# A decoder's start: the first batch of a group handled alone, the rest behind it, in one fixed order

## The chip, the cores and the metric

The kernel runs on one core of a Trainium2 chip. The metric is the device time of one execution in microseconds, as the median of several runs. Five engines work beside each other: TensorE (PE; its weight loads are PEld), VectorE (DVE), ScalarE (ACT), GpSimd (POOL) and SyncE (SP), which here only issues transfers.

## The reference

One decoder layer over 16 batches of 128 tokens with 256 features, all in float32. Each of its three parts is added to its own input:

```
x = x + attn(layernorm(x))          # differential attention, 16 heads
x = x + xattn(layernorm(x), ctx)    # cross attention to ctx, gelu behind it
x = x + ffn(layernorm(x))           # one shared expert, 16 routed ones, best 2 of 16

def attn(x):
    q, k, v = split(x @ W_qkv)      # q, k as 2 * 16 heads of 8; v as 16 heads of 16
    a1 = softmax(q1 @ k1.T * 8**-0.5) @ v
    a2 = softmax(q2 @ k2.T * 8**-0.5) @ v
    o = a1 - lam * a2               # lam from four small vectors
    o = o * rsqrt(mean(o * o) + eps) * subln_w * (1 - lambda_init)
    return o @ W_proj + b_proj
```

The layer norm has no weights: a token's features less their mean, over the root of their variance.

## The kernel before

The 16 batches are 4 groups of 4. A tile has 128 partitions; for a token tile these are the 128 tokens of a batch. `xs[g]` holds group g of x, with one tile in it for each batch.

The start handles group 0 as a whole. `wqkv` is loaded from ScalarE's queue, the four batches of `xs[0]` and then `xs[1]` from SP's. `layernorm` makes each batch's mean and variance on VectorE (`bn_stats`, `bn_aggr`, L124 and L125), adds epsilon (L127), raises the four variances to the power -1/2 on GpSimd (L128), and normalizes batch by batch with a `tensor_scalar` on VectorE (L134) into `xn`. `turns` transposes `xn` on TensorE (L152) and copies it to `xnT`, features by tokens: one half with ScalarE (L155), the other with VectorE (L157). `project` multiplies with the weights `wqk`, whose columns ScalarE has put into another order before (L220). It makes the keys kT (n = 1, copied out by VectorE, L253) and the queries qT (n = 0, scaled and copied out by ScalarE, L255), for each half e of the features. Keys then go by transfers into `kb`, where each head has its own columns between zeros (L260), and into `k3` (L269). Queries go into `qb` (L264), for group 0 from ScalarE's queue. `values` makes `v` (L276, L283). `kb`, `qb`, `v` and `k3` exist twice, for even and odd groups; each is filled with zeros or ones first: `kb0` by VectorE (L206), `kb1` by ScalarE out of the tile `zeros` (L455), the others by GpSimd's `memset` (L207, L210 to L212, L427, L453, L459).

Behind the start runs the loop over steps k. Step k computes for batch k the row maxima of the scores: TensorE's `pq` (L294) and a `tensor_reduce` of VectorE for each (L299), eight of them to a batch. Step k + 1 turns the maxima to a row (`pn`, L307; `nr`, L309) and loads it into `qb` (L311). Step k + 2 makes the probabilities (`pk`, L325, and the exponential, L331), and later steps weigh the values, subtract, normalize and project back. The next group's layer norm, transposes and projections are spread over the four steps of the group before it. Behind the loop come the cross attention, which partly overlaps it, and the two kinds of experts.

Two things set the order on an engine. From `begin = traced()`, just ahead of the loop (L746), `in_order` (called at L1164) ties each instruction on TensorE, VectorE, ScalarE and GpSimd to the one before it in the text. Ahead of `begin` a scheduler picks the order; there `pin` (`keep_in_program_order`) holds some instructions in place, and one fill has a dependency of its own:

```
        filled = pin(nc.gpsimd.memset(ones, 1.0))
        tc.add_manual_dep(
            filled.ins, last_ln.ins.name,
            mybir.DependencyInfo(mybir.DependencyClass.Sync, mybir.DependencyReason.DATA),
            reason="long fills stay behind the first group's normalization",
        )
```

Of the kernel before, what the change touches and what calls it, by code (L numbers as in the profile page):

```python
# [9 lines left out]
F32 = mybir.dt.float32  # L10
# [33 lines left out]
def tile_decoder(  # L44
# [53 lines left out]
    def cons(shape, name, pool=const):  # L98
        return pool.tile(shape, F32, tag=name, name=name)
# [2 lines left out]
        return ap[g * GB : (g + 1) * GB].rearrange("b p d -> p b d")  # L102


    wqkv = cons([P, NC_, 3 * D], "wqkv", aconst)
    nc.scalar.dma_start(out=wqkv, in_=w_qkv.rearrange("(c p) e -> p c e", p=P))
    xs = []
# [7 lines left out]
    make_identity(nc, ident)  # L115
    mhalf = cons([P, 1], "mhalf")
    nc.gpsimd.memset(mhalf, -0.5)
    def statistics(pool, xg, parts=1):

        mv = pool.tile([P, GB, 2], F32, tag="ln_mv", name="ln_mv")  # L120
        rs = pool.tile([P, GB], F32, tag="ln_rs", name="ln_rs")
        for b in range(GB):
            st = pool.tile([P, 6], F32, tag="ln_st", name="ln_st")
            nc.vector.bn_stats(st, xg[:, b, :])  # L124
            nc.vector.bn_aggr(mv[:, b, :], st)  # L125
            if b == GB - 1:
                nc.vector.tensor_scalar(rs, mv[:, :, 1], EPS, None, ALU.add)  # L127
                nc.gpsimd.tensor_tensor(rs, rs, mhalf.to_broadcast([P, GB]), ALU.pow)  # L128
            if (b + 1) % (GB // parts) == 0:
                yield mv, rs  # L130
# [9 lines left out]
    def layernorm(pool, xg, xn):  # L140

        return normalize(xg, xn, *next(statistics(pool, xg)))

    def bank(shape, name):
        return ps.tile(shape, F32, tag="ps", name=name)
# [27 lines left out]
    def traced():  # L173
        return len(nc.cur_bb.bb.instructions)
# [25 lines left out]
    with actx:  # L200
# [3 lines left out]

        zeros = cons([P, 4 * D], "zeros", aconst)
        nc.vector.memset(kbs[0], 0.0)  # L206
        pin(nc.gpsimd.memset(qbs[0], 0.0))  # L207

        def blank_values(n):
            pin(nc.gpsimd.memset(vs[n], 0.0))  # L210
            nc.gpsimd.memset(vs[n][:, :, :, VD : VD + 1], 1.0)
            pin(nc.gpsimd.memset(k3s[n], 1.0))  # L212

        blank_values(0)


        wqk = aconst.tile([P, NC_, 2, D], F32, tag="wqk", name="wqk")
        for n in range(2):
            for c in range(NC_):
                nc.scalar.copy(  # L220
                    wqk[:, c, n, :].rearrange("p (t d j) -> p t d j", d=HD, j=4),
                    wqkv[:, c, n * D : (n + 1) * D].rearrange(
                        "p (t j d) -> p t d j", d=HD, j=4
                    ),
                )

        def normed_tile():
            return share.tile([P, GB, D], F32, tag="xn", name="xn", bufs=1)

        def biased(g):  # L230

            pin(nc.gpsimd.tensor_tensor(
                xs[g], xs[g], bproj_r.unsqueeze(1).to_broadcast([P, GB, D]), ALU.add
            ))

        def turns(g, xn):
            xnT = share.tile([P, NC_, GT], F32, tag="xnT", name="xnT", bufs=1)
            transposed(xn, xnT)
            qT = share.tile([P, NC_, GT], F32, tag="qT", name="qT")
            kT = share.tile([P, NC_, GT], F32, tag="kT", name="kT")  # L240
            return xnT, (qT, kT)

        def project(g, xnT, qk, n, e):

            pp = bank([P, GT], "pp")
            for c in range(NC_):
                nc.tensor.matmul(  # L247
                    pp, lhsT=wqk[:, c, n, e * P : (e + 1) * P], rhs=xnT[:, c, :],
                    start=(c == 0), stop=(c == NC_ - 1),
                )  # L250
            dst = qk[n]
            if n:
                nc.vector.tensor_copy(dst[:, e, :], pp)  # L253
            else:
                nc.scalar.activation(dst[:, e, :], pp, AF.Copy, scale=HD**-0.5)  # L255
            queue = nc.scalar if g == 0 and n == 0 else nc.sync
            kb, qb = kbs[g % 2], qbs[g % 2]
            if n:
                for j in range(4):
                    queue.dma_start(out=kb[j::4, e, j, :], in_=dst[j::4, e, :])  # L260
            else:
                for j in range(4):
                    m = 4 * e + j
                    queue.dma_start(out=qb[m % 3 + 1 :: 4, m, :], in_=dst[j::4, e, :])  # L264
# [6 lines left out]
        def values(g, xnT, b2):  # L271
            pv = bank([P, 2, D], "pv")
            for i in range(2):
                b = 2 * b2 + i
                for c in range(NC_):
                    nc.tensor.matmul(  # L276
                        pv[:, i, :],
                        lhsT=xnT[:, c, b * P : (b + 1) * P],
                        rhs=wqkv[:, c, 2 * D : 3 * D],
                        start=(c == 0),  # L280
                        stop=(c == NC_ - 1),
                    )
            nc.scalar.copy(  # L283
                vs[g % 2][:, 2 * b2 : 2 * b2 + 2, :, 0:VD],
                pv.rearrange("p i (h d) -> p i h d", h=H),
            )

        def maxima(b, c, qT, nm):

            g, i = divmod(b, GB)  # L290
            for t in range(4):
                rows = slice(32 * t, 32 * t + 32)
                pq = bank([P, 4, P], "pq")
                nc.tensor.matmul(  # L294
                    pq, lhsT=qT[rows, c, i * P : (i + 1) * P],
                    rhs=kbs[g % 2][rows, c, :, i * P : (i + 1) * P],
                    start=True, stop=True,
                )
                nc.vector.tensor_reduce(  # L299
                    nm[:, NM * t + 4 * c : NM * t + 4 * c + 4], pq, AX.X, ALU.max, negate=True  # L300
                )
# [98 lines left out]
        def output(b, oT):  # L400
# [6 lines left out]
                )  # L407
            nc.vector.tensor_tensor(xs[g][:, i, :], py, xs[g][:, i, :], ALU.add)

        xn_next = normed_tile()  # L410
        last_ln = layernorm(share, xs[0], xn_next)
        xnT, first = turns(0, xn_next)
        for e in range(NC_):
            for n in (1, 0):
                project(0, xnT, first, n, e)
        for e in range(NC_):
            keys_by_key(0, first[1], e)
        for b2 in range(GB // 2):
            values(0, xnT, b2)


        bproj_r = row(b_proj, D, "bproj_r", aconst)
# [1 line left out]
        wproj = cons([P, NC_, D], "wproj", aconst)  # L424
        wcol = cons([P, 1], "wcol")
        ones = cons([P, P], "ones")
        filled = pin(nc.gpsimd.memset(ones, 1.0))  # L427
        tc.add_manual_dep(
            filled.ins, last_ln.ins.name,
            mybir.DependencyInfo(mybir.DependencyClass.Sync, mybir.DependencyReason.DATA),  # L430
            reason="long fills stay behind the first group's normalization",
        )

        lprod = cons([P, 2, HD], "lprod")
        lsum = cons([P, 2], "lsum")
# [11 lines left out]
        def projection():  # L447

            pin(nc.vector.tensor_scalar(wcol, wcol, 1.0 - LAMBDA_INIT, None, ALU.mult))
            nc.vector.tensor_scalar(wproj, wproj, wcol, None, ALU.mult)  # L450


        pin(nc.gpsimd.memset(zeros, 0.0))  # L453
        for c in range(NC_):
            pin(nc.scalar.copy(  # L455
                kbs[1][:, c].rearrange("p j n -> p (j n)"), zeros[:, 0:1].to_broadcast([P, 4 * GT])
            ))
        blank_values(1)
        pin(nc.gpsimd.memset(qbs[1], 0.0))  # L459
        biased(0)  # L460


        lower = cons([P, P], "lower")
        pin(nc.gpsimd.memset(lower, 1.0))
        nc.gpsimd.affine_select(
            out=lower, in_=lower, pattern=[[1, P]], compare_op=ALU.is_gt, fill=0.0,
            base=0, channel_multiplier=-1,
        )
        eidx = cons([P, NE], "eidx")
        pin(nc.gpsimd.iota(  # L470
            eidx, pattern=[[1, NE]], base=-NE, channel_multiplier=0,
            allow_small_or_imprecise_dtypes=True,
        ))
        carry = cons([P, NE, B], "carry")
        pin(nc.gpsimd.memset(carry, 1.0))
        nc.gpsimd.memset(carry[:, :, 0:1], 0.0)
        tstart = cons([P, NTILE], "tstart")
        pin(nc.gpsimd.iota(
            tstart, pattern=[[P, NTILE]], base=0, channel_multiplier=0,
            allow_small_or_imprecise_dtypes=True,  # L480
        ))

        ebias_r = cons([P, NE], "ebias_r")
        rw = cons([P, NC_, NE], "rw")
# [258 lines left out]

        begin = traced()  # L746
        qk = {0: first}
        nms, probs, ots, as_, diffs, os_ = {}, {}, {}, {}, {}, {}
        for k in range(B + 5):
            g, i = divmod(k, GB)  # L750
            more = k < B and g + 1 < NG
            if k < B:
                nms[k] = work.tile([P, 4 * NM], F32, tag="nm", name="nm")
                maxima(k, 0, qk[g][0], nms[k])
            if k - 1 in nms:
                maxima_rows(k - 1, nms.pop(k - 1))
                for to, of in later.pop(k, ()):
                    load(out=to, in_=of)
# [24 lines left out]
                biased(g + 1)  # L783
            if k < B:
                maxima(k, 1, qk[g][0], nms[k])
            planned(k, 1)
            if k - 3 in ots:
                averaged(ots.pop(k - 3), as_[k - 3][:, 1])
# [457 lines left out]
```

## Time and profile before

| | |
|---|---|
| median of 11 runs | 613.0 us (611.55 to 615.17) |
| the profiled execution | 614.19 us |
| its span, first to last instruction | 612.5 us |
| mean granted TensorE clock | 0.976 |
| PE, PEld | 575.6 us (94%), 386.5 us (63%) |
| DVE, ACT, POOL busy | 304.8 us (50%), 205.9 us (34%), 176.0 us (29%) |

The times of the steps are those of the profiled execution, counted from its first instruction. A line of the timeline gives the start, the duration of a merged run of like instructions, the engine, the line of the kernel, the operation, the tile written and the tiles read, the shapes, the number of instructions (x), and in brackets how long the engine was idle before it and what ended that. A duration starts when the instruction's waits are over. A record of a transfer on a queue (SPq, ACTq) is its issue and not its flow. A float32 matmul of the program shows as two records.

### The profile page before, as it was taken

Reading aid. Unit: us, or ns where it says so; the run is one execution under the profiler, and the core shown is the slowest. Engines: PE = TensorE matmul, PEld = TensorE weight load, DVE = VectorE, ACT = ScalarE, POOL = GpSimd, SP = SyncE. Lnnn points to the kernel's source line nnn. Section 1 sums busy time; section 2 is a strip of 40 time slices with the busy share of each in tenths; the row PEclk is TensorE's granted clock in tenths of the full one; section 3 lists DMA queues with packets and bytes.
Section 4 is the critical chain, followed back from the end, with each engine's and each line's share of the span. In section 5 each row is a group of like instructions: output and inputs, shape, how many; then the busy total and the mean of one; then the engine's idle time right before and its main releaser. Section 6 shows DMA issues by size and latency. Waiting matters only on the chain. (4 is left out here: it accounts for less than half of the span.)

```text
span 612.5 us, 10607 instructions
## 1 busy us (share of the span) xinstructions
PE 575.6 (94%) x3820; PEld 386.5 (63%) x3820; DVE 304.8 (50%) x714; ACT 205.9 (34%) x468; POOL 176.0 (29%) x142
## 2 busy tenths in 40 slices
PE   3989989998999999979799999999899999999996
PEld 1435655654565556666475667465399999988455
DVE  5386866677768773724654543611232232221553
ACT  2325535564454555442425421101122222220110
POOL 8240242244223442541302000676000000004571
PEclk9969989999999999979799999999999999999999
DMA  3311343421104020003300440222499889812352
GB/s 120 111 54 63 101 190 152 154 97 36 54 21 141 3 80 1 2 1 102 105 0 1 118 158 0 77 105 95 130 324 279 280 275 271 252 44 78 102 152 90
DMA packets 58872, 67.65 MB, mean 110 GB/s; under 512 B 8512, under 2 KB 51520, under 8 KB 58816
## 3 DMA queue, kind: packets, MB, share of 16 engines
q1 hardware_dynamic: 55088, 57.21, 28.8%
q0 software_dynamic: 3072, 8.39, 4.3%
q10 hardware_dynamic: 656, 1.31, 0.6%
q8 instruction: 33, 0.54, 0.4%
q14 instruction: 23, 0.19, 0.1%
HBM read 41.73 MB, written 18.61 MB: 99 GB/s over the span
## 5 line engine op out<-in xcount | busy, mean ns | idle before, releaser
L299 DVE TENSOR_REDUCE nm<-pq 128x4 f32<-128x512 f32 x128 | 79.4, 681 | 26.2 <-PE pq L294 26.2
L331 ACT ACTIVATE pr<-pk 128x384 f32<-128x384 f32 (+1 forms) x192 | 70.5, 475 | 19.3 <-PE pk L325 18.8
L1128 POOL DMA_INDIRECT yg<-yd,si x32 | 31.1, 973 | 143.6 <-DMA yd<-yr 128.6
L1101 PE MATMUL pu<-xrT,w 128*128 128x128 f32 x576 | 70.2, 275 | 0.0
L1101 PEld LDWEIGHTS pu<-xrT,w 128*128 128x128 f32 x576 | 67.3, 192 | 0.1
L379 POOL TENSOR_TENSOR rms<-rms,mhalf 128x16 f32<-128x16 f32 x16 | 46.6, 2910 | 71.5 <-DVE rms L378 71.5
L879 PE MATMUL pa<-xT,w 128*128 128x512 f32 x128 | 60.4, 594 | 0.0
L879 PE MATMUL pb<-xT,w 128*128 128x512 f32 x128 | 60.1, 592 | 0.0
L893 PE MATMUL py<-w,h 128*128 128x256 f32 x256 | 55.9, 379 | 0.0
L884 ACT ACTIVATE act<-pa 128x512 f32<-128x512 f32 x32 | 19.1, 597 | 105.2 <-PE pa L879 100.7
L885 DVE TENSOR_TENSOR h<-act,pb 128x512 f32<-128x512 f32 x32 | 21.9, 687 | 63.7 <-PE pb L879 52.7
L893 PEld LDWEIGHTS py<-w,h 128*128 128x128 f32 x256 | 48.6, 190 | 7.9 <-issue 1.4
L325 PE MATMUL pk<-qb,k 32*128 32x384 f32 (+1 forms) x384 | 48.9, 497 | 0.4 <-DVE a L360 0.4
L294 PE MATMUL pq<-kb,qT 32*128 32x512 f32 x256 | 48.6, 640 | 0.6 <-DVE a L360 0.4
L1108 DVE TENSOR_TENSOR hT<-ract,pu 128x256 f32<-128x256 f32 x36 | 15.1, 420 | 63.8 <-ACT ract L1106 63.8
L1063 POOL DMA_INDIRECT xd<-xn,si x32 | 31.1, 972 | 44.3 <-DVE si L1036 34.9
L879 PEld LDWEIGHTS pb<-xT,w 128*128 128x128 f32 x128 | 24.3, 190 | 30.6 <-issue 30.1
L879 PEld LDWEIGHTS pa<-xT,w 128*128 128x128 f32 x128 | 23.7, 190 | 24.6 <-issue 23.9
L247 PE MATMUL pp<-xnT,wqk 128*128 128x512 f32 x64 | 34.9, 682 | 4.0 <-DVE xnT L157 3.5
L1114 PE MATMUL pyr<-w,hT 128*128 x144 | 37.0, 380 | 0.0
L325 PEld LDWEIGHTS pk<-qb,k 32*128 32x128 f32 x384 | 23.3, 185 | 19.7 <-issue 7.1
L349 ACT COPY ot<-po 128x512 f32<-128x512 f32 x32 | 18.8, 586 | 50.1 <-PE po L342 50.1
(157 smaller groups left out, 793.8 us busy)
## 6 DMA issues: line engine op xcount, KB each, us to landing
w<-in_L_ffn_routed_w_dram SPq DMA_DIRECT2D x88, 256.0 KB
xd<-zeros SPq DMA_DIRECT2D x11, 512.0 KB
xr<-xd SPq DMA_DIRECT2D x36, 128.0 KB
yd<-yr SPq DMA_DIRECT2D x36, 128.0 KB
w<-in_L_ffn_shared_w_dram SPq DMA_DIRECT2D x12, 256.0 KB
kb<-kT SPq DMA_DIRECT2D x32, 64.0 KB
k<-kT SPq DMA_DIRECT2D x32, 64.0 KB
ctx<-in_ctx_dram SPq DMA_DIRECT2D x4, 512.0 KB
```

The lines of the kernel that those rows point to most:

```text
L247: nc.tensor.matmul(pp, lhsT=wqk[:, c, n, e * P : (e + 1) * P], rhs=xnT[:, c, :], start=(c == 0), stop=(c == NC_ - 1),)
L294: nc.tensor.matmul(pq, lhsT=qT[rows, c, i * P : (i + 1) * P], rhs=kbs[g % 2][rows, c, :, i * P : (i + 1) * P], start=True, stop=True,)
L299: nc.vector.tensor_reduce(nm[:, NM * t + 4 * c : NM * t + 4 * c + 4], pq, AX.X, ALU.max, negate=True)
L325: nc.tensor.matmul(pk, lhsT=k3s[g % 2][rows, k, i * P : (i + 1) * P], rhs=qbs[g % 2][rows, heads, i * P : (i + 1) * P], start=True, stop=True,
L331: nc.scalar.activation(pr[:, 0:n, :], pk, AF.Exp)
L379: nc.gpsimd.tensor_tensor(rms, rms, mhalf.to_broadcast([P, H]), ALU.pow)
L879: nc.tensor.matmul(pp, lhsT=w[:, c, fs], rhs=xT[g][:, c, :], start=(c == 0), stop=(c == NC_ - 1),)
L893: nc.tensor.matmul(py[:, i, :], lhsT=hs[u][:, f, b * P : (b + 1) * P], rhs=units[u][2][:, f, :], start=(u == 0 and f == 0), stop=(u == NS ...
L1063: i = nc.gpsimd.indirect_dma_start(out=xd[:, :], out_offset=bass.IndirectOffsetOnAxis(ap=slots[n][:, t : t + 1], axis=0), in_=xns[t // GB] ...
L1101: nc.tensor.matmul(pu[:, n, f, :], lhsT=w12[:, c, n, f * P : (f + 1) * P], rhs=xrT[:, c, :], start=(c == 0), stop=(c == NC_ - 1),)
L1114: nc.tensor.matmul(py, lhsT=hT[:, f, :], rhs=w3[:, bass.ds(e * NC_ + f, 1), :], start=(f == 0), stop=(f == NC_ - 1),)
L1128: nc.gpsimd.indirect_dma_start(out=yg, out_offset=None, in_=yd[:, :], in_offset=bass.IndirectOffsetOnAxis(ap=slots[n][:, t : t + 1], axis=0),)
```

## The change

`begin` moves to the first load, so that all instructions on the four engines, those of the start too, stand in the order of the text. The start is written anew in that order. `first_normed([0])` normalizes batch 0 with a power of its own; it is transposed, and eight 128 wide matmuls make its keys and queries in one bank `pp`; its keys are loaded into `kb` by four transfers that hold both halves. `first_normed([1, 2, 3])` follows, and then the transposes and the keys of the three batches, 384 tokens wide. Their queries (`project(0, xnT, first, 0, e, P)`) and the values of the group come inside step 0 of the loop, behind the score matmuls of batch 0. Of the fills, that of `v0` stands behind the power of batch 0, and those of `k30`, `qb0`, `ones` and `zeros` behind the power of the other three; those of the odd tiles (`other_half`) are issued in step 0, the bias of group 0 is added in step 2, and the routing's constants are made in step 4. The dependency of `ones` on the last normalization is gone.

```diff
+    begin = len(nc.cur_bb.bb.instructions)
     wqkv = cons([P, NC_, 3 * D], "wqkv", aconst)
...
-        pin(nc.gpsimd.memset(qbs[0], 0.0))
...
-        def project(g, xnT, qk, n, e):
+        def project(g, xnT, qk, n, e, at=0):
...
         xn_next = normed_tile()
-        last_ln = layernorm(share, xs[0], xn_next)
-        xnT, first = turns(0, xn_next)
+        xnT = share.tile([P, NC_, GT], F32, tag="xnT", name="xnT", bufs=1)
+        first = tuple(
+            share.tile([P, NC_, GT], F32, tag=name, name=name) for name in ("qT", "kT")
+        )
+
+        def first_normed(bs):
+            mv = share.tile([P, GB, 2], F32, tag="ln_mv", name="ln_mv")
+            rs = share.tile([P, GB], F32, tag="ln_rs", name="ln_rs")
+            for b in bs:
+                st = share.tile([P, 6], F32, tag="ln_st", name="ln_st", bufs=2)
+                nc.vector.bn_stats(st, xs[0][:, b, :])
+                nc.vector.bn_aggr(mv[:, b, :], st)
+            part = slice(bs[0], bs[-1] + 1)
+            nc.vector.tensor_scalar(rs[:, part], mv[:, part, 1], EPS, None, ALU.add)
+            nc.gpsimd.tensor_tensor(
+                rs[:, part], rs[:, part], mhalf.to_broadcast([P, len(bs)]), ALU.pow
+            )
+            for b in bs:
+                nc.vector.tensor_scalar(
+                    xn_next[:, b, :], xs[0][:, b, :], mv[:, b, 0:1], rs[:, b : b + 1],
+                    ALU.subtract, ALU.mult,
+                )
+
+        first_normed([0])
+        weights_ordered(1)
+        pt = bank([P, NC_, P], "pt")
+        for c in range(NC_):
+            nc.tensor.transpose(pt[:, c, :], xn_next[:, 0, c * P : (c + 1) * P], ident)
+        nc.scalar.copy(xnT[:, :, 0:P], pt)
+        weights_ordered(0)
+        blank_values(0)
+        first_normed([1, 2, 3])
+        pp = bank([P, 2, NC_, P], "pp")
+        for n in (1, 0):
+            for e in range(NC_):
+                for c in range(NC_):
+                    nc.tensor.matmul(
+                        pp[:, n, e, :], lhsT=wqk[:, c, n, e * P : (e + 1) * P],
+                        rhs=xnT[:, c, 0:P], start=(c == 0), stop=(c == NC_ - 1),
+                    )
+        nc.vector.tensor_copy(first[1][:, :, 0:P], pp[:, 1])
+        for j in range(4):
+            load(out=kbs[0][j::4, :, j, 0:P], in_=first[1][j::4, :, 0:P])
+        nc.scalar.activation(first[0][:, :, 0:P], pp[:, 0], AF.Copy, scale=HD**-0.5)
+        for c in range(NC_):
+            pt = bank([P, GB - 1, P], "pt")
+            for b in range(1, GB):
+                nc.tensor.transpose(
+                    pt[:, b - 1, :], xn_next[:, b, c * P : (c + 1) * P], ident
+                )
+            copies = nc.vector.tensor_copy if c else nc.scalar.copy
+            copies(xnT[:, c, P:].rearrange("p (b t) -> p b t", b=GB - 1), pt)
         for e in range(NC_):
-            for n in (1, 0):
-                project(0, xnT, first, n, e)
+            project(0, xnT, first, 1, e, P)
+        nc.gpsimd.memset(k3s[0], 1.0)
+        nc.gpsimd.memset(qbs[0], 0.0)
         for e in range(NC_):
             keys_by_key(0, first[1], e)
-        for b2 in range(GB // 2):
-            values(0, xnT, b2)
...
-        filled = pin(nc.gpsimd.memset(ones, 1.0))
-        tc.add_manual_dep(
-            filled.ins, last_ln.ins.name,
-            mybir.DependencyInfo(mybir.DependencyClass.Sync, mybir.DependencyReason.DATA),
-            reason="long fills stay behind the first group's normalization",
-        )
+        nc.gpsimd.memset(ones, 1.0)
+        nc.gpsimd.memset(zeros, 0.0)
...
+        def other_half():
+
+            nc.gpsimd.memset(k3s[1], 1.0)
+            for c in range(NC_):
+                nc.scalar.copy(
+                    kbs[1][:, c].rearrange("p j n -> p (j n)"),
+                    zeros[:, 0:1].to_broadcast([P, 4 * GT]),
+                )
+            nc.gpsimd.memset(qbs[1], 0.0)
+            blank_values(1)
...
-        begin = traced()
         qk = {0: first}
...
                 maxima(k, 0, qk[g][0], nms[k])
+            if k == 0:
+                project(0, xnT, first, 0, 0, P)
...
                 maxima(k, 1, qk[g][0], nms[k])
+            if k == 0:
+                project(0, xnT, first, 0, 1, P)
+                values(0, xnT, 0)
+                values(0, xnT, 1)
+                other_half()
+            elif k == 2:
+                biased(0)
+            elif k == 4:
+                routing_constants()
```

More of the change, by code (lines that the diff above doesn't have):

```diff
@@ L206, in tile_decoder, with weights_ordered @@
         nc.vector.memset(kbs[0], 0.0)
-        pin(nc.gpsimd.memset(qbs[0], 0.0))
         def blank_values(n):
-            pin(nc.gpsimd.memset(vs[n], 0.0))
+            nc.gpsimd.memset(vs[n], 0.0)
             nc.gpsimd.memset(vs[n][:, :, :, VD : VD + 1], 1.0)
-            pin(nc.gpsimd.memset(k3s[n], 1.0))
-        blank_values(0)
         wqk = aconst.tile([P, NC_, 2, D], F32, tag="wqk", name="wqk")
-        for n in range(2):
+        def weights_ordered(n):
             for c in range(NC_):
@@ L241, in turns @@
             return xnT, (qT, kT)
-        def project(g, xnT, qk, n, e):
-            pp = bank([P, GT], "pp")
+        def project(g, xnT, qk, n, e, at=0):
+            pp = bank([P, GT - at], "pp")
             for c in range(NC_):
                 nc.tensor.matmul(
-                    pp, lhsT=wqk[:, c, n, e * P : (e + 1) * P], rhs=xnT[:, c, :],
+                    pp, lhsT=wqk[:, c, n, e * P : (e + 1) * P], rhs=xnT[:, c, at:],
                     start=(c == 0), stop=(c == NC_ - 1),
@@ L252, in project @@
             if n:
-                nc.vector.tensor_copy(dst[:, e, :], pp)
+                nc.vector.tensor_copy(dst[:, e, at:], pp)
             else:
-                nc.scalar.activation(dst[:, e, :], pp, AF.Copy, scale=HD**-0.5)
+                nc.scalar.activation(dst[:, e, at:], pp, AF.Copy, scale=HD**-0.5)
             queue = nc.scalar if g == 0 and n == 0 else nc.sync
@@ L259, in project @@
                 for j in range(4):
-                    queue.dma_start(out=kb[j::4, e, j, :], in_=dst[j::4, e, :])
+                    queue.dma_start(out=kb[j::4, e, j, at:], in_=dst[j::4, e, at:])
             else:
@@ L450, in projection, with routing_constants @@
             nc.vector.tensor_scalar(wproj, wproj, wcol, None, ALU.mult)
[L453 to L460, printed above, removed]
-        lower = cons([P, P], "lower")
[L464 to L468, printed above, removed]
+        def other_half():
[7 more added lines that the diff above has]
+            blank_values(1)
+        lower = cons([P, P], "lower")
         eidx = cons([P, NE], "eidx")
[L470 to L473, printed above, removed]
         carry = cons([P, NE, B], "carry")
-        pin(nc.gpsimd.memset(carry, 1.0))
-        nc.gpsimd.memset(carry[:, :, 0:1], 0.0)
         tstart = cons([P, NTILE], "tstart")
[L478 to L481, printed above, removed]
+        def routing_constants():
+            nc.gpsimd.memset(lower, 1.0)
+            nc.gpsimd.affine_select(
+                out=lower, in_=lower, pattern=[[1, P]], compare_op=ALU.is_gt, fill=0.0,
+                base=0, channel_multiplier=-1,
+            )
+            nc.gpsimd.iota(
+                eidx, pattern=[[1, NE]], base=-NE, channel_multiplier=0,
+                allow_small_or_imprecise_dtypes=True,
+            )
+            nc.gpsimd.memset(carry, 1.0)
+            nc.gpsimd.memset(carry[:, :, 0:1], 0.0)
+            nc.gpsimd.iota(
+                tstart, pattern=[[P, NTILE]], base=0, channel_multiplier=0,
+                allow_small_or_imprecise_dtypes=True,
+            )
         ebias_r = cons([P, NE], "ebias_r")
```

## The prediction

> **What bounds the kernel now.** I read the page first: the chain that ended last and the slices.
>
> ```profile
> PE pu L1101 11%; PE pyr L1114 5%; PE py L893 5%; PE pb L879 3%; PE pa L879 3%; PE pxt L1090 1%; DMA xr<-xd 0%; DVE x L1134 0%; DVE x L899 0%; SPq L1080 0%
> ...
> PE   3989989998999999979799999999899999999996
> DVE  5386866677768773724654543611232232221553
> ```
>
> The chain is TensorE work back to 436 us and is lost there, so it doesn't reach the stage that is edited. From the second slice on TensorE is nearly always busy, and its instructions stand in one fixed order. What starts late at the beginning therefore ends late, and the question is only how many microseconds the first 43 us gain or lose. So next came the timeline of that stage, engine by engine.
>
> ```profile
> 8.76 2.52 DVE L134 TENSOR_SCALAR xn<-x,ln_mv,ln_rs 128x256 f32<-128x256 f32 x4 [1.24 <-POOL ln_rs L128]
> ...
> 25.18 4.82 PE L294 MATMUL pq<-kb,qT 32*128 32x512 f32 x24
> ...
> 26.34 2.48 DVE L299 TENSOR_REDUCE nm<-pq 128x4 f32<-128x512 f32 x4 [5.53 <-PE pq L294]
> ```
>
> The first group is normalized by 11.28, TensorE works without a gap from 10.4 to 25.2 (transposes, 16 projection matmuls of 0.85, later 0.43 us, 3.62 us of values), and only then comes the first score matmul, `pq`, at T = 25.18. From the first `tensor_reduce` at 26.34 to 40.2 VectorE never waits: it is the bound there. So the whole kernel moves with T, unless something new ends later behind it.
>
> **What the change could give.** Of the TensorE work ahead of T it moves 3.62 us of values and three quarters of the query projections (8 records at 0.43, so 2.6 of 3.4 us) behind the first reduces, where VectorE is the bound and TensorE has room. It also lets the first batch's keys load alone. T would come earlier if the normalization were done as early as now. I don't think it is, because of the next rows.
>
> ```profile
> 8.70 0.19 POOL L211 MEMSET v<- 128x64 f32 x1
> 8.78 1.39 POOL L212 MEMSET k<- 128x1536 f32 x1
> 11.34 0.20 POOL L427 MEMSET ones<- 128x128 f32 x1 [1.17 <-DVE xn L134]
> ```
>
> A normalizing `tensor_scalar` takes 0.40 us, four in a row 1.37. The first one of the kernel took 1.56: it began at 8.76 and ended at 10.32, 0.15 after GpSimd's fill ended (8.78 + 1.39 = 10.17). The same once more, without a fill:
>
> ```profile
> 299.07 2.41 DVE L134 TENSOR_SCALAR xn<-x,ln_mv,ln_rs 128x256 f32<-128x256 f32 x4
> ...
> 298.02 2.34 POOL L612 TENSOR_TENSOR x<-x,ctx 128x1024 f32<-128x1024 f32 x1
> ```
>
> Four took 2.41 instead of 1.37; GpSimd ended at 300.36, and 300.36 + 0.15 + 3 x 0.32 = 301.47 is their end. So these instructions stand still while GpSimd works. What if GpSimd's next instruction waits for nothing?
>
> ```profile
> 33.38 0.27 DVE L127 TENSOR_SCALAR ln_rs<-ln_mv 128x4 f32<-128x4 f32 x1
> ...
> 31.14 2.34 POOL L232 TENSOR_TENSOR x<-x,bproj_r 128x1024 f32<-128x1024 f32 x1 [11.96 <-DMA bproj_r<-in_L_attn_b_proj_dram]
> 33.42 0.20 POOL L464 MEMSET lower<- 128x128 f32 x1
> ```
>
> GpSimd's add ended at 33.48 and its next fill had begun at 33.42, 0.06 before. VectorE's small instruction (0.17 elsewhere) ended at 33.65, 0.03 after the fill; where one such was held by a single add (295.87 to 296.82) it ended 0.03 after that. So it came in behind both. At 8.76, too, the fill at 8.70 handed over to the one at 8.78. Two hand-overs in two went to GpSimd, though both lay within 0.1 us of VectorE's start.
>
> **The change part by part**, in the times of the profiled execution.
>
> *Batch 0 alone.* Its statistics start at 5.11 as now (its load and the `kb` fill end there). Aggregate, add and hand-over as in the rows of now (0.45, 0.22, 0.32) put the power on GpSimd at 6.10. The power took 1.05 for 4 columns and 2.91 for 16, so 0.155 a column: 0.58 for one, to 6.68. Behind it GpSimd has the fill of `v0` (1.80), begun 0.06 early, so the normalization of batch 0 ends at 6.62 + 1.80 + 0.15 = 8.57. Nothing waits for it yet.
>
> *Batches 1 to 3.* Statistics at a pitch of 0.53 (28.74, 29.29): the third aggregate at 8.5 + 1.06 + 0.45 = 10.0, the add at 10.2, the power at 10.55 for 0.89, to 11.45. GpSimd's next instructions in the new order are `k30`, `qb0`, `ones`, `zeros`, `k31`, `qb1`, `v1`, and none of them waits for anything: the wait of `ones` for the last normalization, which shows above as 1.17 us, is what the diff takes out, and the fills of `k31`, `qb1`, `v1` stand in one row with it. From start to start they take, by the rows of now, 1.34 + 3.45 + 0.15 + 0.89 + 1.34 + 3.45, and `v1` 1.80 to its end: 12.42. Only then does GpSimd wait for itself. If the hand-overs go as the two above, the three normalizations stand from 11.5 to 11.4 + 12.4 = 23.8 and end at 24.0, 24.3 and 24.6, against 11.28 now.
>
> *What hangs on that.* VectorE's order puts the copy of batch 0's keys (done by TensorE since about 10) behind these three, so batch 0 isn't alone at all: copy 24.6 to 25.0 (0.42, the row of L1092). Four loads of `kb` on SP's queue: 2.46 as at 17.13, to 27.45. Landing: at least 0.8 (the traffic of the load issued at 17.13 is over at 18.5), at most 1.95 (`xr<-xd` in the chain); I take the middle, 28.9. Beside it six transposes, two copies and four 384 wide projections at 0.64 a record, cold, end at 28.2, hidden under the landing by 0.7. T = 28.9, which is 3.7 later than now.
>
> *Behind T.* ScalarE now has everything there: queries of e = 0 from T + 2.6 (scores 1.2, projection 1.3 before it), four DMA issues (2.7, as at 19.09), queries and issues of e = 1 to T + 8.9, two value copies (1.1), the two `kb1` fills (3.7): the maxima row `nr` goes out at T + 13.7 instead of T + 7.6. Its four loads issue to T + 16.9 and land at about T + 18.4, while the first `pk` stood at T + 17.6: 0.8 lost. The other edits cost nothing: SP has 4 issues more (2.5 us) but is through with `k3` and `bproj_r` by about T + 10, before `nr`; the adds of the bias and the routing constants move to steps 2 and 4, where GpSimd waited 22.7 us for `o` (L371), and the first user of that `x` comes at step 5. If that cover were gone it would be the 2.3 and 1.2 us that they take.
>
> Sum: 3.7 + 0.8 = 4.5 later. The profiled execution took 614.19 for a span of 612.5; it becomes 618.7. The median of the runs is 613.0, 1.2 below it, so 617.5. The landing (0.6 either way), `nr` (0 to 2) and the clock further down (its half rate stretches at 88, 269 and 300 us can shift, about 1) make 615 to 620.
>
> The Trainium skill, SBUF — State Buffer, section "Who interferes with whom", says that of a VectorE instruction in a two port mode and a GpSimd instruction the first to issue has the shared pair for its whole instruction, and the other is fully blocked. Read literally, for one instruction, it would release the normalization after `k30` alone and make the time of the first rival below; the row at 33.38 speaks for a longer wait.
>
> **The rivals.**
>
> *A: the fill lets go after one instruction (faster).* VectorE asks for 1.3 us before the next fill, not 0.1, and gets in after `k30`: normalizations end at 12.9, 13.3, 13.6, which is 11.0 earlier than in my sum. T = 17.9, 7.3 earlier than now, less the 0.8: 606.5. For it: both hand-overs seen were tight. Against it: they went to GpSimd.
>
> *B: they take turns (faster).* One normalization after `k30`, one after `qb0` (3.51), one after `ones` or `zeros`: the last ends at 16.8 to 17.8, 7.3 earlier than in my sum. T = 21.6, 3.6 earlier, less 0.8: 610.2. It is faster only while `qb0` alone is in between; with `qb1` as well the gain is gone.
>
> *C: the clock stays at half behind T (slower still).* From 30.3 to 40.5 the granted clock is 0.51 now, where TensorE has only scores. The values (3.62 at full clock) and a query projection would take 4 us more there and hold up the scores of batch 1: 621.5. Against it: TensorE is dense from 25.5 on, and at the start the clock rose 4 us after dense work began at 12.6.
>
> *D: nothing.* The moved work was hidden anyway, and the blocked stretch fits under it: 613.
>
> **How the numbers follow.** Chances: my sum 0.62, C 0.06, B 0.15, A 0.14, D 0.03. The likeliest gives 617.5, its own range 615 to 620. Without A and C (0.20) the range goes from B's 610.2, less 1.2 for its own spread, to 620. About 0.2% (1.2 us) is what can be told from no change. Slower: my sum and C less a hundredth, 0.67; same: D and a little of each side, 0.04; faster: A and B, 0.29.
>
> **What would show it.** Right: a first normalization of batches 1 to 3 that begins near 11.5 and lasts about 12 us, with GpSimd's fills in one row above it; the first `pq` near 29; `nr` at about T + 14. Wrong: three normalizations through by 18, which is A or B, told apart by whether the second of them is long; or a first `pq` under 24. If `pq` comes near 29 and the time is still below 613, the stage behind has more slack than I read.

## The result, and the profile after

| | before | after |
|---|---|---|
| median | 612.1 us (610.12 to 615.58, 46 runs) | 620.71 us (619.82 to 623.75, 12 runs) |
| ratio, with its 95% interval | | 1.0145 (1.013 to 1.0159) |
| the profiled execution | 614.19 us | 622.58 us |
| its span | 612.5 us | 620.6 us |
| mean granted clock | 0.976 | 0.983 |
| T, the first score matmul `pq` | 25.18 us | 30.01 us |
| the first `pk` | 42.80 us | 48.90 us |

The kernel became slower by 1.45%. The page of the changed kernel, its chain by line and three engines in 40 slices:

```profile
PE pu L1160 10%; PE pyr L1173 5%; PE py L952 4%; PE pa L938 3%; PE pb L938 3%; PE pxt L1149 1%; DMA xr<-xd 0%; DVE x L1193 0%; DVE x L958 0%; SPq L1139 0%
...
PE   2499998998999999979799999999899999999996
...
DVE  7785686676757875634654433711132222310553
POOL 5521152234233242433402000577000000004572
```

The chain says as little as before. The slices say where to look: TensorE's first two are 2 and 4 where they were 3 and 9, and VectorE's go from 5 and 3 to 7 and 7. VectorE isn't doing more work there; its instructions last longer. The timeline of VectorE:

```profile
6.64 1.87 DVE L429 TENSOR_SCALAR xn<-x,ln_mv,ln_rs 128x256 f32<-128x256 f32 x1 [0.77 <-POOL ln_rs L425]
...
11.31 13.08 DVE L429 TENSOR_SCALAR xn<-x,ln_mv,ln_rs 128x256 f32<-128x256 f32 x3 [0.98 <-POOL ln_rs L425]
24.31 0.41 DVE L451 COPY kT<-pp 128x256 f32<-128x256 f32 x1
...
31.17 2.48 DVE L298 TENSOR_REDUCE nm<-pq 128x4 f32<-128x512 f32 x4 [0.49 <-PE pq L293]
...
39.74 2.48 DVE L298 TENSOR_REDUCE nm<-pq 128x4 f32<-128x512 f32 x4 [1.36 <-PE pq L293]
```

The second line holds the change's loss: three instructions of 0.4 us took 13.08. The copy of batch 0's keys, which TensorE had long made, stands behind them. GpSimd in the same stretch:

```profile
10.41 0.87 POOL L425 TENSOR_TENSOR ln_rs<-ln_rs,mhalf 128x3 f32<-128x3 f32 x1 [1.74 <-DVE ln_rs L424]
11.22 1.38 POOL L465 MEMSET k<- 128x1536 f32 x1
12.53 3.51 POOL L466 MEMSET qb<- 128x4096 f32 x1
15.99 0.20 POOL L476 MEMSET ones<- 128x128 f32 x1
16.13 0.95 POOL L477 MEMSET zeros<- 128x1024 f32 x1
17.03 1.38 POOL L499 MEMSET k<- 128x1536 f32 x1
18.35 3.51 POOL L505 MEMSET qb<- 128x4096 f32 x1
21.80 1.80 POOL L211 MEMSET v<- 128x2048 f32 x1
23.66 0.24 POOL L212 MEMSET v<- 128x64 f32 x1
```

No fill has a bracket, so none waited for another engine; each begins a little before its neighbour ends, until 23.60 (21.80 + 1.80), where the last one waits for the one before it, into whose tile it writes. The three normalizations end at 24.39, which is 23.60 + 0.15 + 2 x 0.32: the first got in at that first pause. TensorE then:

```profile
25.56 4.52 PE L246 MATMUL pp<-xnT,wqk 128*128 128x384 f32 x8
30.01 1.14 PE L293 MATMUL pq<-kb,qT 32*128 32x512 f32 x8
31.08 1.56 PE L246 MATMUL pp<-xnT,wqk 128*128 128x384 f32 x4
32.57 1.14 PE L293 MATMUL pq<-kb,qT 32*128 32x512 f32 x8
33.64 1.56 PE L246 MATMUL pp<-xnT,wqk 128*128 128x384 f32 x4
35.03 3.62 PE L275 MATMUL pv<-wqkv,xnT 128*128 128x256 f32 x16
38.58 1.14 PE L293 MATMUL pq<-kb,qT 32*128 32x512 f32 x8
...
45.30 2.39 PE L246 MATMUL pp<-xnT,wqk 128*128 128x512 f32 x4 [0.96 <-ACT xnT L157]
```

The first `pq` has no wait either: TensorE was busy with the keys of batches 1 to 3, eight records, until it began. So the loads of batch 0's keys into `kb` didn't set T; those projections did. The loads were issued until 27.41:

```profile
24.75 2.66 SPq L194 DMA_DIRECT2D kb<-kT  x4
```

In the first experiment below, where TensorE was through in time and waited for these loads, the first `pq` stood 1.31 behind their last issue (16.08 to 17.39). By that they had landed here at about 28.7 (an estimate). Behind T TensorE is dense for 8.57 us until the scores of batch 1 at 38.58. VectorE was ready for them earlier and waited 1.36 (the last line of its fence). ScalarE is late as well:

```profile
40.92 3.71 ACT L501 COPY kb<-zeros 128x2048 f32<-128x2048 f32 x2
44.52 0.25 ACT L308 COPY nr<-pn 32x128 f32<-32x128 f32 x1
44.67 0.57 ACT L157 COPY xnT<-pt 128x512 f32<-128x512 f32 x1
```

The row of maxima and the next group's `xnT` stand behind the two fills of `kb1`; TensorE's 0.96 at 45.30 is the wait for that copy. Whether it costs anything, the experiments say.

### The profile page after: what moved, and what is told of

It is laid out like the page before. It is cut to its first block, busy times and chain, and to the rows that moved or that the text cites. A ratio compares the mean times of both kernels' runs of the same rounds, so it can differ in the third digit from the quotient of the medians.

```text
span 620.6 us, 10649 instructions
## 1 busy us (share of the span) xinstructions
PE 575.8 (93%) x3836; PEld 388.5 (63%) x3836; DVE 318.4 (51%) x716; ACT 206.2 (33%) x470; POOL 176.1 (28%) x143
## 3 DMA queue, kind: packets, MB, share of 16 engines
q10 hardware_dynamic: 656, 1.31, 0.6%
## 5 line engine op out<-in xcount | busy, mean ns | idle before, releaser
L938 PE MATMUL pa<-xT,w 128*128 128x512 f32 x128 | 62.1, 608 | 0.0
L938 PEld LDWEIGHTS pb<-xT,w 128*128 128x128 f32 x128 | 24.5, 192 | 31.2 <-issue 30.7
L246 PE MATMUL pp<-xnT,wqk 128*128 128x512 f32 (+1 forms) x64 | 31.4, 619 | 5.5 <-DVE xnT L159 4.0
```

The lines of the kernel that those rows point to most:

```text
L246: nc.tensor.matmul(pp, lhsT=wqk[:, c, n, e * P : (e + 1) * P], rhs=xnT[:, c, at:], start=(c == 0), stop=(c == NC_ - 1),)
L938: nc.tensor.matmul(pp, lhsT=w[:, c, fs], rhs=xT[g][:, c, :], start=(c == 0), stop=(c == NC_ - 1),)
```

## The experiments

The theory is that of the prediction: GpSimd holds VectorE's normalization off through its whole row of fills, and all else follows from T. Theory two is the first rival's: a fill lets go when it is over. The comparison of runs goes by ratio to the kernel before on the same chip; of the traces, T and the first `pk` are compared. The diffs are against the changed kernel where nothing else is said.

**The fills behind the normalization.** One dependency is added, nothing is moved.

```diff
-        nc.gpsimd.memset(k3s[0], 1.0)
+        filled = nc.gpsimd.memset(k3s[0], 1.0)
+        tc.add_manual_dep(filled.ins, last_ln.ins.name, ...)   # last of batches 1 to 3
```

> The changed kernel with one dependency more: the fill of k30, and with it the row of GpSimd's fills behind it, waits for the last normalization of batches 1 to 3. Theory (the row of fills shuts VectorE out of SBUF): the three normalizations take about 1.05 us in place of 13.08 and end near 12.4; TensorE's half-rate transposes and projections then carry on to a first pq near 18 to 19.5 in place of 30.0; about 607, so 4 to 6 below the kernel before. Rival (the order itself, a key copy behind three normalizations and the work put behind T, costs what was lost): pq comes earlier but the time stays above 615.

609.71 us, ratio 0.9958 (0.9938 to 0.9977). Its timeline:

```profile
11.31 1.06 DVE L429 TENSOR_SCALAR xn<-x,ln_mv,ln_rs 128x256 f32<-128x256 f32 x3 [0.98 <-POOL ln_rs L425]
12.44 1.38 POOL L466 MEMSET k<- 128x1536 f32 x1 [1.16 <-DVE xn L429]
17.39 1.14 PE L293 MATMUL pq<-kb,qT 32*128 32x512 f32 x8 [0.31 <-issue]
27.12 2.48 DVE L298 TENSOR_REDUCE nm<-pq 128x4 f32<-128x512 f32 x4 [1.39 <-PE pq L293]
```

The three take 1.06 instead of 13.08, T comes 12.6 earlier than in the changed kernel, and the kernel is 0.4% faster than before instead of 1.45% slower. That the hold is what moves T is shown. The size was expected larger (4 to 6 us, about 607): T is 7.8 earlier than before and the first `pk` (37.54) only 5.3, so what lies behind T gives 2.5 back, and the median shows 3.2 (612.93 on this chip to 609.71). Of the 2.5, 1.3 go with the clock: the next group's projection took 3.66 at half rate here, 2.39 in the changed kernel.

**Half of the row behind.** The same dependency, on the fill of `k31` instead of `k30`.

> The changed kernel, where only the second half of the row (k31, qb1, v1) waits for the last normalization; k30, qb0, ones, zeros stay behind the power. Theory: the block ends with zeros, 11.22 + 5.86 = 17.1, the three normalizations last about 6.6 in place of 13.08, pq 6.4 earlier, time about 6.4 less than the changed kernel, near 614. Rival (VectorE gets in whenever one fill ends and the long time came from something else): no change against the changed kernel, near 620.

615.27 us, ratio 1.004 (1.0015 to 1.0065).

```profile
11.31 6.56 DVE L429 TENSOR_SCALAR xn<-x,ln_mv,ln_rs 128x256 f32<-128x256 f32 x3 [0.98 <-POOL ln_rs L425]
16.13 0.95 POOL L478 MEMSET zeros<- 128x1024 f32 x1
17.93 1.38 POOL L500 MEMSET k<- 128x1536 f32 x1 [0.84 <-DVE xn L429]
```

GpSimd now waits behind `zeros`, at 17.08, and the three end at 17.87. The hold grows and shrinks with the row up to GpSimd's first wait, through four fills here and seven there. T is 23.45, 6.6 earlier than in the changed kernel, as expected, and 1.7 earlier than before; the first `pk` (42.34) is 0.5 earlier than before, and yet the median is 2.3 longer. Where that is lost isn't shown: the profiled execution, 612.83, is the shortest of the ten.

**The kernel before without its one dependency.** Nothing of the change is in it.

```diff
         filled = pin(nc.gpsimd.memset(ones, 1.0))
-        tc.add_manual_dep(filled.ins, last_ln.ins.name, ...)
```

> The kernel before with one thing taken out: the dependency of the fill of ones on the last normalization. Nothing else differs, save that the scheduler puts ones one place earlier. Theory: the first normalization ends with v1's fill, near 13.1 in place of 10.32. If VectorE then keeps the port for all four, pq is 2.8 later, near 615; if GpSimd takes it back after one (the fills of k31 and qb1 follow), it is some 7.8 later, near 620. Rival (fills cost one instruction each at most): the time stays within 1 us of before.

621.38 us, ratio 1.0123 (1.0093 to 1.0152): 8.5 us from one dependency. T is 32.81.

```profile
9.01 9.84 DVE L134 TENSOR_SCALAR xn<-x,ln_mv,ln_rs 128x256 f32<-128x256 f32 x4 [1.24 <-POOL ln_rs L128]
...
11.41 1.79 POOL L210 MEMSET v<- 128x2048 f32 x1
13.26 0.24 POOL L211 MEMSET v<- 128x64 f32 x1
13.35 1.44 POOL L212 MEMSET k<- 128x1536 f32 x1
14.73 3.65 POOL L454 MEMSET qb<- 128x4096 f32 x1
13.41 0.47 PE L152 MATMUL pt<-ident,xn 128*128 128x128 f32 x1 [13.41 <-DVE xn L134]
14.99 0.48 PE L152 MATMUL pt<-ident,xn 128*128 128x128 f32 x1 [1.10 <-DVE xn L134]
18.58 1.54 PE L152 MATMUL pt<-ident,xn 128*128 128x128 f32 x6 [3.12 <-DVE xn L134]
```

The transposes show when each normalization was through. The first came out at 13.4, in the pause behind `v` (13.20, where GpSimd waits for its own fill). The hand-over to `k`, 0.1 later, went to GpSimd. The second normalization got in at the next one: 14.99 is behind the fill of `k` (14.79). 18.58 is behind that of `qb` (18.38), the end of the row. So VectorE got no turn before GpSimd's first wait and one at a hand-over behind it. The expectation had this as its second case (T some 7.8 later; it is 7.6), but not the rule behind it: no turn at all before a wait.

**All fills behind, that of `v0` too.** The first experiment, and `blank_values(0)` moved behind the fill of `qb0`.

> As the first of these four, and the fill of v0 goes behind the other two even tiles as well, so that no fill stands beside any normalization. Theory: batch 0's normalization takes 0.40 in place of 1.87, batches 1 to 3 follow 1.4 earlier; pq near 17 to 18, time about 605.5, 1 to 1.5 below the first. Rival (TensorE's half-rate work sets pq, not the normalization): the same time as the first within 0.5.

607.92 us, ratio 0.9934 (0.9898 to 0.9971). The normalization of batch 0 takes 0.41 instead of 1.87, T is 16.09, the first `pk` 36.31; the median is 1.8 below the first experiment's. What it costs is one row, because GpSimd's row now ends later:

```profile
23.53 1.80 POOL L211 MEMSET v<- 128x2048 f32 x1
24.26 1.10 DVE L129 TENSOR_SCALAR ln_rs<-ln_mv 128x4 f32<-128x4 f32 x1
```

That instruction takes 0.17 elsewhere. It ends at 25.36, just behind the fill (25.33). Even four columns are held, 0.93 here.

**One fill cut in 32.** Is it the length of an instruction, or the row?

```diff
-        nc.gpsimd.memset(qbs[0], 0.0)
+        for m in range(8):
+            for i in range(GB):
+                nc.gpsimd.memset(qbs[0][:, m, i * P : (i + 1) * P], 0.0)
```

> The changed kernel with the fill of qb0 cut into 32 fills of 128 columns (0.15 us apart, 4.8 in all); nothing else. Question: which fills go ahead of a normalization that is asking. Theory one (GpSimd keeps the port as long as it has no wait of its own): the three normalizations stand through the whole row, now 1.3 longer, and take about 14.4 us in place of 13.08. Theory two (only the fills that GpSimd had already taken up when VectorE asked go first, some 7 or 8 of them): the first normalization gets in behind k30 and some 6 or 7 small fills, near 13.6, the other two behind as many again each; 4 to 6 us for the three, and pq 8 us earlier.

One run, 623.39 us (before on that chip: 614.02).

```profile
11.31 14.35 DVE L429 TENSOR_SCALAR xn<-x,ln_mv,ln_rs 128x256 f32<-128x256 f32 x3 [0.99 <-POOL ln_rs L425]
...
12.54 4.78 POOL L468 MEMSET qb<- 128x128 f32 x32
```

38 fills with 37 hand-overs between them, and none went to VectorE. The row got 1.27 longer and the hold with it. Shorter instructions didn't help.

**One pause.** A small fill of a part of `k30` behind the fill of `k30`, so that GpSimd waits once for itself.

```diff
         nc.gpsimd.memset(k3s[0], 1.0)
+        nc.gpsimd.memset(k3s[0][:, 0, 0:64], 1.0)
```

> The changed kernel with one small fill more, of 64 columns of k30, behind the fill of k30: it writes where that one wrote, so GpSimd waits there for its own end once, and the rest of the row follows without a wait. Theory one (VectorE gets in only where GpSimd waits, and then for one instruction): the first normalization ends at 12.8, the other two stand to the end of the row near 24, three in about 13. Theory two (once in, VectorE gets a turn at every hand-over, as the transposes in e3_before_no_wait hint, at 13.4, 15.0 and 18.6): second behind qb0 near 16.4, third near 16.7; three in about 5.4, pq near 22.5. Theory three (once in, it keeps the port for all three): three in about 2.2.

One run, 636.48 us. This chip, on which the second form of "the work back" and "both kernels again" ran too, took some 20 us longer for the kernel before (634.32), so only ratios within it and the traces of the start are compared.

```profile
11.32 5.40 DVE L429 TENSOR_SCALAR xn<-x,ln_mv,ln_rs 128x256 f32<-128x256 f32 x3 [0.99 <-POOL ln_rs L425]
...
12.66 0.18 POOL L466 MEMSET k<- 128x64 f32 x1
12.75 3.51 POOL L467 MEMSET qb<- 128x4096 f32 x1
16.20 0.34 POOL L477 MEMSET ones<- 128x128 f32 x1
16.49 1.12 POOL L478 MEMSET zeros<- 128x1024 f32 x1
```

5.40 instead of 13.08, from 0.06 us of pause. The fills that follow have VectorE's turns in them: `ones` takes 0.34 instead of 0.20, `zeros` 1.12 instead of 0.95. One normalization came in at the pause, none at the hand-over 0.1 later, one behind `qb0` (12.75 + 3.51 = 16.26), one behind `ones`. This is what the third experiment suggested. Why there is no turn ahead of the first pause stays open.

**The zeros of `kb1` early.** On top of "all fills behind", ScalarE makes them ahead of the first group's query copies, where it is idle, out of a tile that is there by then.

```diff
+        for c in range(NC_):
+            nc.scalar.activation(
+                kbs[1][:, c].rearrange("p j n -> p (j n)"),
+                mhalf.to_broadcast([P, 4 * GT]), AF.Copy, scale=0.0,
+            )
...
-                nc.scalar.copy(kbs[1][:, c]..., zeros[:, 0:1].to_broadcast(...))
```

> The version without any fill beside a normalization (e4_all_free), with the two fills of kb1 (3.71 us on ScalarE, between the value copies and nr) made earlier, ahead of the first query copy, as a copy scaled by zero. Theory (ScalarE's chain behind T costs about 1 us: TensorE waits 0.99 for the copy of xnT at 30.79): nr goes out 3.5 us earlier, xnT's copy is no longer late, the first pk comes 0.9 earlier, 0.9 less than e4_all_free. Rival (nr and xnT lie under other work): no difference beyond 0.3 up to the first pk.

606.0 us, ratio 0.9882 (0.9855 to 0.9909). `nr` goes out at 27.48 instead of 30.64, and the first `pk` stands at 35.40, 0.91 earlier, though T was 0.42 later. That is the size that was expected, but not for the expected reason:

```profile
31.08 1.12 PE L246 MATMUL pp<-xnT,wqk 128*128 128x512 f32 x2 [0.24 <-ACT xnT L157]
33.06 1.13 PE L246 MATMUL pp<-xnT,wqk 128*128 128x512 f32 x2 [0.86 <-DVE xnT L159]
```

TensorE still waits 1.10 in all (0.99 before), now for VectorE's half of `xnT`. What got shorter is the projection itself: 2.25 at full clock, where it took 3.68 at half in "all fills behind". And from T to the first `pk` it is 18.89, the same as in the changed kernel, which has the fills on ScalarE and full clock there. So the rival, that `nr` and `xnT` lie under other work, isn't refuted, and how much of this version's gain is ScalarE's isn't shown.

**The values one step later.** On top of that, the values of group 0 stand behind the row of maxima of batch 0 in step 1, instead of ahead of the scores of batch 1.

```diff
+            if k == 1:
+                values(0, xnT0, 0)
+                values(0, xnT0, 1)
             if k < B:
                 maxima(k, 1, qk[g][0], nms[k])
             if k == 0:
+                xnT0 = xnT
                 project(0, xnT, first, 0, 1, P)
-                values(0, xnT, 0)
-                values(0, xnT, 1)
```

> The same as e7_early_zeros, and the values of the group (3.6 us of TensorE) moved once more, from behind the scores of batch 0 to between pn and the second scores of batch 1. Theory (behind T TensorE is the bound up to batch 1, 8.6 us of work where VectorE takes 8.3): VectorE's wait for the third pq (0.45 here, 1.39 where no fill hid it) goes; 0.4 to 1.4 less than e7_early_zeros. Rival (the values then hold up the transposes of the next group): 0 to 2 more.

604.01 us, ratio 0.9857 (0.9835 to 0.9879), 2.9% of the kernel before under the changed one by the two ratios. It beats both kernels.

```profile
23.75 3.62 PE L275 MATMUL pv<-wqkv,xnT 128*128 128x256 f32 x16
24.76 2.48 DVE L298 TENSOR_REDUCE nm<-pq 128x4 f32<-128x512 f32 x4
```

The same 3.62 us of TensorE now lie under VectorE's reduces, and the reduces of batch 1 have no bracket: their wait (0.86 in the version that this one is built on, 1.36 in the changed kernel) is gone. The first `pk` stands at 33.94, 1.46 earlier, with the same T and full clock in both.

**The work back ahead of T.** How much of the gain is the early batch, and how much the work behind T? On top of "all fills behind", the query projections and values of batches 1 to 3 return ahead of the first `pq`.

> The version without fills beside a normalization (e4_all_free), with the queries and the values of batches 1 to 3 put back ahead of the first pq, as in the kernel before; batch 0 is still normalized, projected and loaded alone. Theory (the gain of the change is this work behind T, under VectorE's reduces): first pq near 22 in place of 16.1, first pk near 39.8 in place of 36.3, so 3.5 more than e4_all_free and about 2 to 3 less than the kernel before. Rival (the gain is batch 0's early start alone): the same as e4_all_free within 1.

618.65 us, ratio 1.0082 (1.0051 to 1.0113). This one missed its question. The fills of `qb0` and `v0` stood in the text behind what writes there, so group 0's queries and values were overwritten by the fills, and GpSimd's row waited 13.21 us:

```profile
25.57 3.51 POOL L475 MEMSET qb<- 128x4096 f32 x1 [13.21 <-DMA k<-kT]
```

T was 22.16 as expected, but the next group's power was late behind that row, and the first `pk` stood at 47.55. The fills were moved ahead of the projections, and it was run again:

> What e9_work_back was meant to be: no fill beside a normalization, batch 0 alone, and the queries and values of batches 1 to 3 ahead of the first pq as in the kernel before, with the fills ahead of the loads that write into them. Theory (what pays is the work put behind T): first pq near 22.2, first pk near 39.8, 3.5 more than e4_all_free and about 2 to 3 less than the kernel before. Rival (the early start of batch 0 pays): as e4_all_free within 1.

633.28 us, ratio 0.9984 (0.9945 to 1.0023), which can't be told from no change. T is 22.16 again, the first `pk` 39.60: 3.0 earlier than in the kernel before on that chip (42.60), and 3.3 later than with the work behind T (36.31). So in these traces about half of what the early start is worth comes from the batch alone and half from the work that moved behind it. The median shows 1.0 of the 3.0, with an interval from 3.5 less to 1.5 more.

**Both kernels again,** on the chip of the longer runs, for how much one execution differs from another.

> The kernel before once more, for a second trace of it: of the 8.6 that the change costs, 6.1 are there at 66 us and the rest comes later, in stretches where the granted clock is at half in one trace and not in the other. If that belongs to one execution and not to the kernel, this trace has its stretches behind 64 us elsewhere, and the same instructions lie up to 2 us from those of the first trace. If it belongs to the kernel, they lie within 0.3.

> The changed kernel once more, for a second trace of it, with the same question: at 66 us it should lie 6.1 behind the kernel before, within 0.3, whatever the clock does later; the half-rate stretches at 151.8 and 445.4 come again only if they belong to the kernel.

631.58 and 647.39 us. The normalizations take 13.08 again. T is 24.05 and 30.70, the first `pk` 42.60 and 49.66: 7.1 apart, where the first pair was 6.1 apart, so the expected 6.1 within 0.3 isn't met. The start of the kernel before moved by 1.1 at T and 0.2 at `pk` between two executions, that of the changed kernel by 0.7 and 0.8: TensorE's projections ahead of T took 9.20 and 7.79 in the one, 4.52 and 5.20 in the other. Both later stretches that the expectation names came again in the changed kernel: 151.8 at 153.2, and 445.4 at 467.3, where the same instructions stand 22.1 later. Neither trace of the kernel before has one at these instructions.

## Why the prediction was right and wrong

Predicted 617.5 (range 609 to 620, slower at 0.67); measured 620.71. The direction and the mechanism of the hold are right, and the time lies 0.7 outside the range. In the profiled execution the working gave 618.7, and it took 622.58, so 3.9 is missing. Three terms failed: the projections ahead of T were counted half, the loss behind T was put down to the wrong wait, and the clock further down was put at nothing. The steps:

**The row of fills: right, to half a microsecond.** Batch 0's normalization was put to end at 8.57 and ended at 8.51; the power of the other three was put at 10.55 for 0.89 and stood at 10.41 for 0.87; the three normalizations were put from 11.5 to 24.6 and stood from 11.31 to 24.39. The sum of start-to-start rows (12.42) was good because the fills take the same time wherever they stand. The first four experiments show that it is the cause, from both sides. To go from two hand-overs, each within 0.1 us of VectorE's start, to a row of 13 us was a guess, though (its chance was put at 0.62), and partly luck: in the third experiment and with one pause VectorE got hand-overs, so one pause early in the row would have undone the sum (5.40 instead of 13.08).

The Trainium skill, SBUF — State Buffer, section "Who interferes with whom", gives the port pair that the two engines share to whoever issues first, for the whole instruction. In these runs the hold was one instruction long only once VectorE had come in (5.40 with a pause); ahead of that it lasted through 7 fills (13.08) and through 38 (14.35).

**T: the first step that failed.** The projections of the keys of batches 1 to 3 were written as "four 384 wide projections at 0.64 a record, cold, end at 28.2, hidden under the landing by 0.7". A float32 matmul of the program shows as two records, so the four are eight, and they took 4.52 (25.56 to 30.08) instead of 4 x 0.64 = 2.56. The term was 1.96 too small. Not hidden, they became what T waits for: T = 30.01, where the sum had 28.9, so 1.1 is left of it, some three tenths of the miss. The trace of before had the count: its 16 records of `pp` are the 8 projection matmuls of the program, of keys and queries, two halves and two parts of the features each. TensorE's rate is in that term too: in the first experiment, where TensorE wasn't idle for 10 us ahead of them, the same eight records took 2.85. In the second execution of the changed kernel they took 5.20, and T was 30.70, which is the sum with the count put right (25.6 + 8 x 0.64 = 30.7). The landing, 28.9 in the sum and about 28.7 by the runs, was right.

**Behind T: the size near, the wait wrong.** The sum had 0.8 here, for a `nr` that goes out late; from T to the first `pk` it was 17.62 before and is 18.89, so 1.27. `nr` is late as forecast (T + 13.7 in the sum, T + 14.5 in the trace), but it isn't what the first `pk` waits for: `pk` has no wait ahead of it, and in "the zeros of `kb1` early" `nr` goes out at T + 11.0 and T to `pk` is the same 18.89. TensorE's 0.96 for `xnT` doesn't count either, since the projection needs VectorE's half of `xnT` too, and that is there only at 46.51 (45.83 + 0.68). What the sum didn't have is VectorE's wait of 1.36 for the scores of batch 1, behind TensorE's 8.57 us from T on. Without the values ahead of these scores T to `pk` falls to 17.43, below that of the kernel before. The 20.22 of "all fills behind" is about this 18.89 with the next group's projection at half rate (3.68 instead of 2.39).

**The clock further down: put at nothing, and not settled.** The sum had nothing for it and the range about 1. From the first `pk` on the changed kernel's profiled execution takes 571.7, the one before 569.7, so 2.0 more. That goes with the half rate stretches. From the first `pk` to the end of TensorE's work they add up to 20.5 us in the changed kernel's trace and to 17.1 in that of before. Eight more traces come from the two chips that run the kernel before in 613 to 614 us: with 13.7 us (three traces) the stage took 567.8 to 568.8, with 17.1 (four) 569.9 to 570.1, and with 20.5 (one) 570.2. Against the trace of before, the changed kernel loses 1.3 at the stretch at 151.8 and 1.8 at the one at 445.4, and gains 1.6 around 308, where its stretch is half as long.

All these stretches begin in one of TensorE's five waits of more than 1.5 us, or at most 2.3 us behind one. In the changed kernel the waits end at 95.8, 150.6, 279.4, 306.6 and 445.1, and each has its stretch, in both executions; the kernel before has three of them in one execution and two in the other. The waits are about as long in both kernels (2.2 and 1.8, 1.8 and 1.8, 4.5 and 4.5, 3.0 and 3.0, 2.4 and 2.3 us), so their length alone doesn't decide it. What does, and so whether the 2.0 belong to the kernel's new order, these runs don't show. The medians lie 8.6 apart (8.0 to 9.7 by the interval) and the first `pk` 6.1 to 7.1, so the typical execution loses something down there too.

**The rivals.** A (one fill, then free) falls with the 13.08, and with the 37 hand-overs. B (turns) falls for this kernel, yet it is what happens behind a pause; its sum for the normalizations, an end at 16.8 to 17.8, is close to what the kernel with one pause shows (16.72). C (half rate behind T) didn't come: the values took 3.62 and the query projections 0.39 a record, at full clock. D (nothing) falls by the interval.

1.1 at T, 0.5 behind it and 2.0 further down make 3.6 of the 3.9; the other 0.3 is time outside the span. A range with 1.1 for the records' count and 2 instead of 1 for the clock would have ended at 622 instead of 620.

## What to carry to other kernels

Before fills are moved on GpSimd, look at what VectorE does in the same microseconds: a row of fills without a wait in it stopped normalizations and even an add of four columns for as long as the row lasted, so the row belongs behind the critical instructions, with a dependency if the order alone doesn't hold it there. That dependency was worth 8.5 us in the old order and some 11 in the new. When an order is rewritten, carry over what its dependencies protected; and when work is moved behind the point that sets the pace, put it under the engine that is the bound there, not ahead of that engine's next input.

## What the runs showed of the hardware

- The hold of GpSimd's fills over VectorE's normalizations lasts until GpSimd first waits, however its row is cut: 13.08 us for 7 fills, 14.35 for 38, 6.56 for the first four. Behind a wait VectorE got the pause, not the hand-over 0.1 us later, and then the next ones: 5.40 with one 0.06 us pause, and the three dates 13.4, 15.0 and 18.6 in the old kernel without its dependency.
- Half rate stretches of TensorE's clock, 3.4 us or a multiple of it, follow short waits of TensorE in a dense kernel (1.8 to 4.5 us), at the same few instructions in every trace; which of the shorter waits get one differs from trace to trace. In the ten traces apart from the slow chip 3.4 us more of them went with some 1 to 1.5 us more time, on average.
- One of the chips ran the kernel before in 634.32 us at the median, others in 612.93 and 614.02. In its trace that is one place:

```profile
422.45 2.93 PE L893 MATMUL py<-w,h 128*128 128x256 f32 x6 [17.16 <-issue]
```

TensorE stands still for 17.16 us in the middle of `py`, where the first trace has no wait. Up to 390 us the trace runs 2.4 ahead of the first, and from 420 on 17.4 behind it. The clock is at half for 17.1 us from 410.2, so mostly inside that wait. The other three traces of this chip have waits of 10.2 us or more in `py` as well, and none of the ten of the other chips has one there. What TensorE waits for, the profile doesn't show.
